# When the bias rows, exponents, mask pieces and last sources of a ranked graph propagation are issued

## The chip, the cores and the metric

The kernel runs on one core of a Trainium2 chip. The metric is device time in microseconds (us) of one execution. One execution is also recorded by the hardware profiler, and its page and trace are the evidence that is read here.

Engines are named as in the profile: PE is TensorE's matmuls, PEld its weight loads, DVE is VectorE, ACT is ScalarE, POOL is GpSimd, and SP is SyncE, which only issues loads here. Each engine takes its own instructions in order; between engines there are semaphores.

## The reference, cut to what matters

A graph of N = 3327 nodes has a sparse, weighted, symmetric-pattern adjacency matrix A (3327 x 3327, f32) and node features x (3327 x 64). Four residual layers follow one another, each `x = x + f(relu(layernorm(x)))`. In all, A or a matrix made from it multiplies a 64-wide array eight times; I call these propagations k = 0 to 7.

- Layer 0, k = 0 and 1: two gated graph steps, each A times features, then a GRU cell.
- Layer 1, k = 2: each nonzero is replaced by a power of one half that depends on its rank in its row:

```
mask = (adj != 0)
rank = cumsum(mask, axis=1); deg = rank[:, -1:]
k = minimum(deg, 100); pos = rank - (deg - k)
w = mask * where(pos > 0, 0.5 ** (k - pos), 0)
out = w @ (input @ weight) + bias
```

- Layer 2, k = 3, 4, 5: the weights are A squared element by element; each step is `x = (w @ x) @ W.T + b`.
- Layer 3, k = 6 and 7: plain A again, with a small dense step and a tanh.

## The kernel before, in words

**Tiles and chunks.** The targets are cut into four chunks of 384, 384, 384 and 512 columns per half (`CH`), two halves each. Chunks 0 and 1 are group 0, chunks 2 and 3 are group 1 (`GROUPS`). A tile holds 128 sources against all targets of one group: 128 x 2 x 384 columns a chunk, 768 KB in group 0 and 896 KB in group 1. Twenty slots hold tiles; SP loads them from HBM in the order of use, each as soon as its slot is free. A is read anew for every pair of propagations.

**Units.** A list of units (k, chunk, tile) is written out by the functions `alone` and `joint`: group 0 at k = 0; group 1 at k = 0 and 1; group 0 at k = 1 and 2; group 1 at k = 2 and 3; and so on. `joint(g, k, sweep, later, keep)` lets the second propagation follow the first: a tile is used for k and, `later` tiles afterwards, for k + 1. The function `run` plays the list. Ahead of a unit's matmuls it issues loads, the preparation of tiles (squares for k = 3 to 5, L404 on ACT), the exponents of the ranked units (`expand`, three units ahead), and mask pieces.

**A ranked unit (k = 2).** A tile's mask is made by two "pieces" on DVE (L427: adj != 0, as bf16, one per half), and POOL fetches one row of totals into it by DMA (L432). PE multiplies the mask by a triangle of ones (L271, `tri`), which gives ranks in a PSUM bank, one for each of the two halves s. ACT (L482) or DVE (L480) turns a bank into a bf16 power of two, `e`, and frees the bank; the choice is `on_vector`. PE then does L566: six matmuls, three bf16 terms of y by two halves. The last piece of a tile frees the tile's slot, and so releases a load.

**Last sources.** Each 128-source tile loses its last source to the totals row. Those 26 sources are handled once per group by `last_sources(g)`: POOL clears a half slot (L523), SP loads 26 rows for each half (two L527), DVE forms the mask and subtracts totals (L529, L533), and ACT makes the exponents (L535). They are used by a unit called `SPECIAL`, the last k = 2 unit of a chunk. The two runs of `last_sources` are tasks that start 70 and 140 us into the planner's own time.

**Tasks.** What follows a finished sum is a generator with a planned delay at each `yield`: `spend` lets time pass as units are issued, `advance` takes one step, `finish` takes all that are left. After k = 1 comes `gru`, which sets y[2] and, 80 planned us later in group 1 (14 in group 0), adds a row of biases to xs (`add_row`, L802). After k = 2 comes `after_2`: evacuate the sum (L711 on DVE or L709 on ACT), a dense step on PE (L271 with `bd`), add to xs (L796), layernorm (L774 to L776 and L782, L783 on DVE, L779 squares on ACT, L785 power on POOL, L789 on DVE, which sets y[3]), and 15 planned us later another `add_row`. The corresponding steps of the layer before are L794 (residual), L781 and L859 to L868 (splitting y into three bf16 terms).

**The order around the change.** A `SPECIAL` unit needs y of all chunks. It therefore finishes the tasks of all other chunks before its matmuls, also what their `yield`s would have left for later. The pieces are spread by `run`: in k = 2, one per unit in group 1, none while group 0 works on its own sources, except every third unit once y[2] of group 0 is there.

Of the kernel before, what the change touches and what calls it, by code (L numbers as in the profile page):

```python
# [52 lines left out]
NC = 4  # L53
PARTS = (4, 5)
CWM = 512
GROUPS = [(0, 1), (2, 3)]
# [23 lines left out]
SPECIAL = None  # L80
# [16 lines left out]
def kernel(  # L97
# [165 lines left out]
    def width(c):  # L263
        return blocks(c) * P
# [60 lines left out]
    def begin(c, task):  # L325
        finish(c)
        tasks[c] = [task, 0.0]
        advance(c)

    def finish(c):  # L330
        while c in tasks:
            advance(c)

    def later_task(us, task):
        yield us
        yield from task
# [10 lines left out]
    y = [[None] * NC for _ in range(8)]  # L347
# [54 lines left out]
    def square(sq, v, turn):  # L402
        if turn % 3 or any(ch in tasks or (2, ch) in sums for ch in range(NC)):
            nc.scalar.activation(sq, v, AF.Square)  # L404
        else:
            nc.vector.tensor_tensor(sq, v, v, ALU.mult)  # L406

    def prepare(k, c, t):

        if t is SPECIAL:  # L410
            return
        kind = KIND[k] if k != COUNT else COUNT
        if kind in (RANKED, COUNT) and t.mask is None:
            make_mask(t, kind)
        if kind == SQUARED and t.in_place and c not in t.squares:
            t.squares.add(c)
            square(t.view(c), t.view(c), t.q + c)

    pieces = deque()

    def make_mask(t, kind):

# [15 lines left out]
    def mask_pieces(n=0, t=None):  # L438

        while pieces and (n > 0 or any(u is t for u, _, _ in pieces)):  # L440
            _, half, piece = pieces.popleft()
            piece(half)
            n -= 1

    def expand(k, c, t):

        if k == COUNT:
            return None
        w = width(c)
        if t is SPECIAL:  # L450
            g = c // 2
            w0 = (CH[c][0] - CH[GROUPS[g][0]][0]) * P
            finish(NC + 1 + g)
            return lastw[g][:, w0:w0 + w].bitcast(BF16)
        if KIND[k] == PLAIN or (KIND[k] == SQUARED and t.in_place):
            return t.view(c)
        if KIND[k] == SQUARED:
            room = Mask(t.w)
            wide = room.view.rearrange("p s w -> p (s w)").bitcast(F32)[:, :2 * w].rearrange("p (s w) -> p s w", s=2)
            square(wide, t.view(c), t.q + c)  # L460
            squared[k, c, t] = room
            return wide
        wide = work.tile([P, 2, CWM], I16, name="e", bufs=4)[:, :, :w]

        mask_pieces(t=t)
        for s in range(2):
            i, ps = take()  # L470
            mm(ps[:, :w], tri, t.mask.view[:, s, t.cols(c)])
            own = chunk_of(t.q % NB) in GROUPS[t.g]
            busy = any((k - 1, ch) in sums for ch in GROUPS[t.g])
            if t.g == 1 and not own and any(y[3][ch] is None for ch in GROUPS[0]):

                on_vector = s and c == GROUPS[1][1]
            else:
                on_vector = s and (own if t.g == 0 and (own or busy) else c == GROUPS[t.g][1] or t.g == 1 and not own)
            if on_vector:
                nc.vector.tensor_scalar(wide[:, s], ps[:, :w], BITS, 0.0, op0=ALU.add, op1=ALU.max)  # L480
            else:
                nc.scalar.activation(wide[:, s], ps[:, :w], AF.Relu, bias=bitsb)  # L482
            give(i)
        spend(STREAM_US * w / CWM * 0.5)
        if c == GROUPS[t.g][1]:
            t.mask.free()
        return wide.bitcast(BF16)
# [29 lines left out]
    def last_sources(g):  # L517

        w = sum(width(c) for c in GROUPS[g])
        w0 = CH[GROUPS[g][0]][0] * P  # L520
        room = Mask(w)
        v = room.view.rearrange("p s w -> p (s w)").bitcast(F32)
        nc.gpsimd.memset(v, 0.0)  # L523
        yield 4.0
        rows = adjT.rearrange("(q p) (s n) -> q p s n", p=P, s=2)
        for s in range(2):
            nc.sync.dma_start(out=v[s * D:s * D + NQ], in_=rows[:, P - 1, s, w0:w0 + w])  # L527
        yield 12.0
        nc.vector.tensor_scalar(v, v, 0.0, 129.0 * TWO7, op0=ALU.not_equal, op1=ALU.mult)  # L529
        for c in GROUPS[g]:  # L530
            finish(("count", c))
        yield 1.0
        nc.vector.scalar_tensor_tensor(v, totals[g], -TWO7, v, op0=ALU.mult, op1=ALU.add)  # L533
        yield 1.5
        nc.scalar.activation(lastw[g], v, AF.Relu, bias=bitsb)  # L535
        room.free()

    def propagate(k, c, t, rhs, first, last):
        if k == COUNT:
            count(t, first, last)  # L540
            return
        w = width(c)
        if first:
            sums[k, c] = [take(sums=True) for _ in range(2 if k == 7 and c == PARTS[1] else 1)]
            sums[k, c] = [sums[k, c][0], sums[k, c][-1]]
        acc = sums[k, c]
        if t is SPECIAL:
            for ch in range(NC):
                if ch != c:
                    finish(ch)  # L550
            terms = [[lasty[:, h, i, :] for h in range(2)] for i in range(3)]
            rhs = [rhs, rhs]
        else:
            s, b = divmod(t.q, NB)
            cs = chunk_of(b)
            if y[k][cs] is None:
                finish(cs)
            terms = [[yk[:, b - CH[cs][0], s, :]] * 2 for yk in (y[k][cs] if KIND[k] == RANKED else [y[k][cs]])]
            rhs = [rhs[:, h, :] for h in range(2)]
            if KIND[k] != RANKED:  # L560
                t.used()
            if (k, c, t) in squared:
                squared.pop((k, c, t)).free()
        for n, yq in enumerate(terms):
            for h in range(2):
                nc.tensor.matmul(acc[h][1][h * D:(h + 1) * D, :w], yq[h], rhs[h], start=first and n == 0,  # L566
                                 stop=last and n == len(terms) - 1)
        if t is not SPECIAL and t.early and t.mask is None:
            make_mask(t, RANKED)
        spend(STREAM_US * w / CWM * (0.75 if KIND[k] == RANKED else 1.0))  # L570
        if last:
            begin(c, after[k](c, sums.pop((k, c))))
# [97 lines left out]
    def run():  # L670
        total = {}
        for k, c, t in units:
            total[k, c] = total.get((k, c), 0) + 1
        done = {}
        loaded, masked, prepared, expanded = 0, 0, 0, deque()
        for i, (k, c, t) in enumerate(units):
            while loaded < len(units) and loaded < i + LOAD:
                u = units[loaded][2]
                if u is not SPECIAL and u.slot is None:
                    if len(dead) <= RESERVE and loaded > i + EXPAND:  # L680
                        break
                    u.load()
                loaded += 1
            while masked < min(loaded, i + MASK):
                if is_masked(*units[masked]):
                    if not spare and len(dead) <= RESERVE + 1:
                        break
                    make_mask(units[masked][2], RANKED)
                masked += 1
            while prepared < min(loaded, i + PREPARE):  # L690
                prepare(*units[prepared])
                prepared += 1
            while len(expanded) < min(EXPAND + 1, len(units) - i):
                assert prepared > i + len(expanded)
                expanded.append(expand(*units[i + len(expanded)]))
            if k != 2:
                mask_pieces(1 + len(pieces) // 6)
            elif not (c in GROUPS[0] and (t is SPECIAL or chunk_of(t.q % NB) in GROUPS[0])):
                mask_pieces(1)
            elif i % 3 == 0 and all(y[2][ch] is not None for ch in GROUPS[0]):  # L700
                mask_pieces(1)
            n = done[k, c] = done.get((k, c), 0) + 1
            propagate(k, c, t, expanded.popleft(), n == 1, n == total[k, c])

# [260 lines left out]
    alone(0, 0, sweep=2, lag=5)  # L965
    joint(1, 0, sweep=6, later=4, keep=3, lag=2)
    joint(0, 1, sweep=4, later=20, keep=0)
    joint(1, 2, sweep=6, later=5, keep=1)
    joint(0, 3, sweep=8, later=4, keep=4)
    joint(1, 4, sweep=8, later=4, keep=4)  # L970
    joint(0, 5, sweep=8, later=4, keep=4)
# [6 lines left out]
        else:  # L978
            begin(c, before_0(c))
    begin(NC, more_constants())  # L980
    begin(NC + 1, later_task(70.0, last_sources(0)))
    begin(NC + 2, later_task(140.0, last_sources(1)))
    run()
    for c in list(tasks):
        finish(c)
# [39 lines left out]
```

## Time and profile before

The median of three runs is 712.32 us (712.25 to 713.13).

| what | value |
|---|---|
| profiled execution | 712.98 us |
| span of its trace | 710.9 us |
| mean granted PE clock | 0.999 |
| PE busy | 682.9 us, 96% of the span |
| DVE busy | 338.7 us, 48% |
| ACT busy | 267.4 us, 38% |
| POOL busy | 79.5 us, 11% |
| HBM read | 199.45 MB, 282 GB/s over the span |

Busy shares by stage, from the windows of the trace (us busy of the stretch):

| stretch, us | what runs | PE | DVE | ACT | DMA share |
|---|---|---|---|---|---|
| 200 to 220 | group 0, k = 1 ends; GRU cells begin | 19.75 | 17.62 | 10.31 | 0.95 |
| 220 to 240 | group 0, k = 2; GRU cells | 19.64 | 17.28 | 15.01 | 0.90 |
| 240 to 260 | group 0, k = 2 | 19.93 | 16.51 | 15.99 | 0.56 |
| 260 to 280 | group 1, k = 2 begins; after_2 of chunks 0 and 1 | 17.13 | 17.54 | 12.98 | 0.44 |
| 280 to 300 | group 1, k = 2 and 3 | 17.97 | 15.71 | 16.37 | 0.52 |
| 380 to 620 | k = 3 to 6 | 240.00 of 240 | 72.87 | 84.59 | 0.80 |

How to read it: ends of matmuls are modelled, so PE's busy time is an upper view of it, and what matters is where PE starts late. L numbers are lines of the kernel before. In the trace's lines the tiles of the PSUM banks are called `sum` and `temp`, whatever they hold.

### The profile page before, as it was taken

The page shows a single profiled execution, that of the slowest core. Times are in us where ns is not written, and L with a number is a line of the kernel's source. Part 1 is how long each engine was busy: PE and PEld are TensorE (multiplying, and loading weights), DVE is VectorE, ACT ScalarE, POOL GpSimd, SP SyncE. Part 2 cuts the span into 40 slices and gives each one's busy share as a digit, 9 for nine tenths or more (in the row PEclk, how much of TensorE's full clock was granted, in tenths as well). Part 3 has the DMA queues.
Part 4 walks back from the last instruction along what each step waited for, and adds up shares of the span by engine and source line. Part 5 has one row for each costly group of instructions (what it writes and reads, how often), then busy time and mean ns, then how long its engine had stood idle before and what let it go on. Part 6 is the DMA issues. An engine that isn't in the chain of part 4 may idle for free.

```text
span 710.9 us, 12617 instructions
## 1 busy us (share of the span) xinstructions
PE 682.9 (96%) x5128; PEld 353.9 (50%) x5128; DVE 338.7 (48%) x692; ACT 267.4 (38%) x411; POOL 79.5 (11%) x114
## 2 busy tenths in 40 slices
PE   1999999999999998999999999999999999999997
PEld 1454666643546785446444444334444444334464
DVE  7456826643997888747533103221271565005101
ACT  1014100122137868788997224740166600000101
POOL 4300000001383414011100000000010000000000
PEclk9999999999999999999999999999999999999999
DMA  9999995189699833682799659962997399927991
GB/s 343 401 388 405 405 401 175 53 319 395 197 326 324 290 123 106 236 282 90 271 372 348 233 175 409 406 239 94 385 366 266 111 390 405 405 80 270 404 401 38
DMA packets 68549, 201.31 MB, mean 283 GB/s; under 512 B 7228, under 2 KB 8228, under 8 KB 68492
## 3 DMA queue, kind: packets, MB, share of 16 engines
q1 hardware_dynamic: 65596, 199.46, 75.9%
q8 instruction: 40, 0.66, 0.4%
q10 hardware_dynamic: 720, 0.85, 0.3%
q0 software_dynamic: 2176, 0.20, 0.2%
q14 instruction: 17, 0.14, 0.1%
HBM read 199.45 MB, written 0.85 MB: 282 GB/s over the span
## 4 chain that ended last, share of the span: by engine, by line
PE 57%; DVE 3%; DMA 1%; ACT 1%; issue 0%; POOL 0%; ACTq 0%; DVEq 0%; POOLq 0%; SPq 0%
PE sum L566 53%; PE temp L271 3%; PE temp L730 1%; DMA adj<-in_adjT 1%; DVE e L480 1%; DVE adj L427 1%; POOL st L785 0%; DVE both L765 0%; ACT both L764 0%; DVE st L774 0%; ACT e L482 0%; DVE xs L796 0%; PE sum L271 0%; DVE st L782 0%; ACT adj L404 0%
## 5 line engine op out<-in xcount | busy, mean ns | idle before, releaser
L566 PE MATMUL sum<-adj,y 128*64 128x384 f32 (+3 forms) x3016 | 532.4, 502 | 3.1 <-DVE e L480 1.6
L566 PEld LDWEIGHTS sum<-adj,y 128*64 128x64 f32 x3016 | 228.8, 137 | 251.0 <-issue 222.3
L404 ACT ACTIVATE adj<-adj 128x768 f32<-128x768 f32 (+1 forms) x174 | 142.7, 891 | 49.6 <-PE sum L566 23.9
L427 DVE TENSOR_SCALAR adj<-adj 128x768 bf16<-128x768 f32 (+3 forms) x208 | 113.3, 593 | 39.0 <-PE temp L501 35.0
L566 PE MATMUL sum<-e,both 128*64 128x384 bf16 (+1 forms) x624 | 73.1, 339 | 0.4 <-DVE e L480 0.2
L482 ACT ACTIVATE e<-temp,bitsb 128x384 int16<-128x384 f32 (+1 forms) x117 | 66.2, 607 | 18.6 <-PE temp L271 13.5
L764 ACT COPY both<-sum 64x384 f32<-64x384 f32 (+3 forms) x17 | 8.1, 477 | 150.3 <-PE sum L566 150.3
L765 DVE COPY both<-sum 64x384 f32<-64x384 f32 (+3 forms) x17 | 9.7, 568 | 114.6 <-ACT both L764 113.4
L406 DVE TENSOR_TENSOR adj<-adj 128x768 f32<-128x768 f32 (+1 forms) x34 | 32.6, 1008 | 53.3 <-DMA adj<-in_adjT 31.0
L785 POOL TENSOR_TENSOR st<-st,mhalf 128x6 f32<-128x6 f32 (+1 forms) x16 | 24.3, 1516 | 291.1 <-DVE st L783 291.1
L271 PE MATMUL temp<-adj,tri 128*64 128x384 bf16 (+1 forms) x334 | 50.8, 341 | 0.2
L432 POOL DMA_DIRECT2D adj<-totals x52 | 37.0, 714 | 124.3 <-DMA adj<-in_adjT 74.8
L566 PEld LDWEIGHTS <-both 128*64 128x64 bf16 x624 | 40.6, 110 | 19.2 <-issue 6.7
L480 DVE TENSOR_SCALAR e<-temp 128x384 int16<-128x384 f32 (+1 forms) x50 | 30.5, 611 | 21.1 <-PE temp L271 9.8
L271 PEld LDWEIGHTS <-tri 128*64 128x64 bf16 x416 | 28.1, 110 | 17.9 <-issue 10.0
L759 DVE STREAM_TRANSPOSE both<-y 32x96 f32<-32x96 f32 (+1 forms) x128 | 35.6, 278 | 2.9
L711 DVE COPY t<-sum 128x384 f32<-128x384 f32 x8 | 4.4, 556 | 61.2 <-PE sum L566 61.2
L501 PE MATMUL temp<-adj,behind 128*64 128x384 bf16 x208 | 30.1, 339 | 0.9 <-DVE adj L427 0.7
L501 PEld LDWEIGHTS <-behind 128*64 128x64 bf16 x208 | 16.8, 110 | 17.7 <-issue 16.5
L709 ACT COPY t<-sum 128x384 f32<-128x384 f32 (+1 forms) x8 | 4.2, 528 | 53.9 <-PE sum L566 53.9
L921 DVE TENSOR_TENSOR y<-temp,brow 128x384 f32<-128x384 f32 (+1 forms) x8 | 4.7, 591 | 29.6 <-PE temp L271 29.6
L535 ACT ACTIVATE lastw<-adj,bitsb 128x768 int16<-128x768 f32 (+1 forms) x2 | 2.0, 990 | 44.7 <-DVE adj L533 44.7
(121 smaller groups left out, 329.2 us busy)
## 6 DMA issues: line engine op xcount, KB each, us to landing
adj<-in_adjT SPq DMA_DIRECT2D x130, 768.0 KB, 8.9
adj<-in_adjT SPq DMA_DIRECT2D x104, 896.0 KB, 11.1
xs<-in_x SPq DMA_DIRECT2D x1, 640.0 KB, 4.2
adj<-totals POOLq DMA_DIRECT2D x26, 3.0 KB, 5.7
adj<-totals POOLq DMA_DIRECT2D x26, 3.5 KB, 3.1
out<-xs ACTq DMA_DIRECT2D x2, 192.0 KB
out<-xs ACTq DMA_DIRECT2D x1, 256.0 KB, 6.7
stage<-in_weights SPq DMA_DIRECT2D x2, 112.0 KB, 14.3
```

Of the source, the lines that this page charges most:

```text
L271: nc.tensor.matmul(out[hs], lhsT[:, hs], rhs, start=start, stop=stop)
L404: nc.scalar.activation(sq, v, AF.Square)
L406: nc.vector.tensor_tensor(sq, v, v, ALU.mult)
L427: nc.vector.tensor_scalar(t.mask.view[:rows, half], t.view()[:rows, half], 0.0, None, op0=ALU.not_equal)
L432: nc.gpsimd.dma_start(out=t.mask.view[P - 1:P], in_=totals[t.g][t.q:t.q + D + 1:D, :])
L480: nc.vector.tensor_scalar(wide[:, s], ps[:, :w], BITS, 0.0, op0=ALU.add, op1=ALU.max)
L482: nc.scalar.activation(wide[:, s], ps[:, :w], AF.Relu, bias=bitsb)
L501: nc.tensor.matmul(counts[c][1][s * D:(s + 1) * D, :w], behind[:, NQ - 1 - t.q:NQ - 1 - t.q + D], t.mask.view[:, s, t.cols(c)], start=firs ...
L566: nc.tensor.matmul(acc[h][1][h * D:(h + 1) * D, :w], yq[h], rhs[h], start=first and n == 0, stop=last and n == len(terms) - 1)
L759: nc.vector.transpose(to[at:at + 32, :, q], h[q * 32:(q + 1) * 32, :, s, f * 32:(f + 1) * 32])
L765: nc.vector.tensor_copy(both[c][upper(1), 1], acc[1][1][upper(1), :width(c)])
L785: nc.gpsimd.tensor_tensor(st[:, 3, :n], st[:, 2, :n], mhalf[:, :n], ALU.pow)
```

## The change

1. `SPECIAL`: instead of finishing all tasks of the other chunks, each chunk's task is advanced only until its y is set. The bias rows (`add_row`) are left to their planned time.
2. Exponents: a flag `relief["squares"]` is set when the first in-place squares are issued, and takes the place of the test on y[3] of group 0. A flag `relief["pieces"]` is set for the own ranked units of group 0 after y[2] of that group is there; while it is set, an s = 1 bank goes to DVE unless (q + c) is divisible by 4.
3. In those units a piece is issued every second unit, not every third.
4. `joint(1, 2)`: k = 3 follows k = 2 six tiles later, not five.
5. `last_sources` begin at 130 and 155 of planned time, not 70 and 140.

```diff
@@ prepare
         if kind == SQUARED and t.in_place and c not in t.squares:
             t.squares.add(c)
+            relief["squares"] = True
             square(t.view(c), t.view(c), t.q + c)
 
     pieces = deque()
+
+    relief = {"squares": False, "pieces": False}
@@ expand
-            if t.g == 1 and not own and any(y[3][ch] is None for ch in GROUPS[0]):
+            if t.g == 1 and not own and not relief["squares"]:
 
                 on_vector = s and c == GROUPS[1][1]
+            elif relief["pieces"]:
+                on_vector = s and (t.q + c) % 4
             else:
@@ propagate
         if t is SPECIAL:
             for ch in range(NC):
-                if ch != c:
-                    finish(ch)
+                while y[k][ch] is None:
+                    advance(ch)
@@ run
+            relief["pieces"] = False
             if k != 2:
                 mask_pieces(1 + len(pieces) // 6)
             elif not (c in GROUPS[0] and (t is SPECIAL or chunk_of(t.q % NB) in GROUPS[0])):
                 mask_pieces(1)
-            elif i % 3 == 0 and all(y[2][ch] is not None for ch in GROUPS[0]):
-                mask_pieces(1)
+            elif all(y[2][ch] is not None for ch in GROUPS[0]):
+                relief["pieces"] = t is not SPECIAL
+                if i % 2 == 0:
+                    mask_pieces(1)
@@ the list of units and tasks
-    joint(1, 2, sweep=6, later=5, keep=1)
+    joint(1, 2, sweep=6, later=6, keep=1)
-    begin(NC + 1, later_task(70.0, last_sources(0)))
-    begin(NC + 2, later_task(140.0, last_sources(1)))
+    begin(NC + 1, later_task(130.0, last_sources(0)))
+    begin(NC + 2, later_task(155.0, last_sources(1)))
```

## The prediction

> **What bounds the kernel now.** I read the page's busy times first, then what TensorE (PE) waits for, then PE, DVE, ACT and the DMA queue in order of time in the stretches where PE waits.
>
> ```profile
> PE 682.9 (96%) x5128; PEld 353.9 (50%) x5128; DVE 338.7 (48%) x692; ACT 267.4 (38%) x411; POOL 79.5 (11%) x114
> ```
>
> PE carries the kernel: a gain is lost PE time won back. Ends of matmuls are modelled, so I count losses from starts: six bf16 matmuls of 384 columns follow one another in 0.49 us (287.20 to 287.69), four f32 ones in 0.64 (289.09 to 289.73). A start later than that spacing allows is lost time. Over the execution this gives some 20 us beside the 14.9 of the first wait; 380 to 620 us lose nothing, 120 to 345 us lose about 12. The waits for PE:
>
> ```profile
> PE temp L747 <- DVE y L789: 14.9, 1, 14.9
> PE sum L271 <- DVE e L480: 2.1, 2, 1.1
> PE sum L566 <- DVE e L480: 1.8, 2, 1.6
> PE sum L566 <- DMA adj<-in_adjT: 0.9, 2, 0.7
> ...
> PE temp L271 <- DVE t L711: 0.8, 1, 0.8
> ```
>
> Columns: total, times, longest. Apart from the first, the large ones belong to DVE in the ranked pass (k=2), and one to a load. By spacing: 0.83 at 130.41 (load), 0.37 at 212.89 (load), 0.95 at 264.18 (L711), 1.24 at 273.44, 1.23 at 278.62, 0.49 at 280.95, 0.43 at 282.75, 1.81 at 286.29 (exponents, L480 and L482). What DVE does before them (start, duration, work, wait before it):
>
> ```profile
> 262.41 1.16 DVE L802 TENSOR_TENSOR xs<-xs,brow 128x384 f32<-128x384 f32 x2
> 263.48 0.55 DVE L711 COPY t<-sum 128x384 f32<-128x384 f32 x1
> ...
> 271.75 0.56 DVE L789 SCALAR_TENSOR_TENSOR y<-t,st 128x384 f32<-128x384 f32 x1 [1.54 <-POOL st L785]
> 272.23 0.55 DVE L802 TENSOR_TENSOR xs<-xs,brow 128x384 f32<-128x384 f32 x1
> 272.70 0.68 DVE L480 TENSOR_SCALAR e<-sum 128x512 int16<-128x512 f32 x1
> ...
> 277.88 0.68 DVE L480 TENSOR_SCALAR e<-sum 128x512 int16<-128x512 f32 x1
> ...
> 285.55 0.68 DVE L480 TENSOR_SCALAR e<-sum 128x512 int16<-128x512 f32 x1
> ```
>
> Three bias additions (L802) and a layernorm end (L789), none of them urgent, stand ahead of L711 and L480, which PE awaits. L711's sum was complete at 261.79, the rank product for 272.70 at 269.33.
>
> **What the Trainium skill says.** "Perfetto Trace Analysis", Identifying the Most-Contended Engine, holds matmul busy share a poor measure of nearness to the limit; the trace agrees: 96% covers a busy figure that includes modelled ends. Its section Optimization Strategy says to find the gaps of the bounding engine by stage and what posts their semaphore: that is the list above. Its section Matmuls wants independent groups rotated through PSUM banks so that evacuation overlaps; here the rotation is what fails, since PE waits at 273.44 and 278.62 for a bank that L480 has not emptied. "DMA: Bandwidth & Descriptors", Issuing engines are not separate DMA queues, has all issuers share 16 DMA engines; the trace agrees where it matters: 407 GB/s and a share of 1.04 in 205 to 210 us.
>
> **The change part by part.**
>
> *Last sources' rows, first group, later.* Its two L527 loads leave 97 us for about 172, and the half slot with them. The last four 896-wide loads before 130 us then start when their slots come free (98 to 119) and land by about 124.7, where the late one landed at 130.36. The 0.83 at 130.41 goes. Its L529 and L533 (about 0.53 and 0.95 us to the next start) now fall at 200 to 202 us, in a full DVE (4.96 of 5 us in 200 to 205), ahead of the pieces L427 that free slots for the last 768-wide loads. The last of these is issued at 205.76 after a piece at 205.15, so up to 1.5 us later; but DMA is backlogged until it lands at 212.8 and has two 91 KB loads less, and PE comes 0.83 earlier. Bounds of the loss there: 0 (backlog covers all) to 1.5 (landing moves with the piece). I take 0.3.
>
> *Second group later.* Its L527 pair goes behind the 768-wide loads and holds SP until POOL's memset (L523, queued behind the copies L868 to 216 us). Queued behind are 896-wide loads (208.48 to 219.38 before) first read by pieces at 250: cover of 25 us, cost nothing; uncovered it would be up to 8 us. L529 and L533 leave 209 to 211.5 for here:
>
> ```profile
> 229.81 0.56 DVE L843 TENSOR_TENSOR adj<-adj 128x384 f32<-128x384 f32 x1
> ...
> 232.13 0.55 DVE L480 TENSOR_SCALAR e<-sum 128x384 int16<-128x384 f32 x1
> ...
> 233.85 0.56 DVE L480 TENSOR_SCALAR e<-temp 128x384 int16<-128x384 f32 x1
> 234.33 0.55 DVE L794 SCALAR_TENSOR_TENSOR xs<-temp,xs 128x384 f32<-128x384 f32 x1
> ```
>
> DVE has no gap, and PE starts 0.05 or 0.06 us after the ends of the L480 at 232.13, 233.85 and 236.18 and the L794. L529 (0.54) goes in before 228.06, where 0.22 of waiting and rounding absorb 0.3: +0.24. L533 (1.0) goes in after 232.13 and passes whole to PE at 234.47: +1.0. ACT's L535 (1.04) waits for it and blocks ACT from 232.8 to 234.9; the L482 behind it are late by 1.7 against banks that PE, itself 1.24 late, asks for at least 0.4 later: nothing. Sum +1.24; bounds 0.2 (L533 absorbed) and 2.3 (L535 adds its 1.04).
>
> *Exponents shared.* Four L480 of 384 between 253 and 260 us move to ACT as L482 (0.47 each to the next start). PE spends 0.813 us per 384-wide unit there, and ACT starts within 0.1 of its input; each moved one makes ACT at most 0.5 late, and banks come round after more than 1. Cost nothing; uncovered, 4 x 0.47.
>
> *Pieces every second unit.* They use the DVE time freed: five L427 of 896 (0.53 each) come into 250 to 265 us and leave 265 to 291. POOL gets two L432 before each L785, whose inputs PE finished at 260: nothing.
>
> *Bias rows not forced.* The L802 at 262.41, 262.88 and 272.23 (0.47, 0.60, 0.47) go to 295 to 303 us, where DVE is a third idle. Now DVE in the new order, with the start-to-start times of the old one (L480 0.47 or 0.60, L427 0.53, L796, L774 and L782 0.58, L776 and L789 0.48):
> - L711 starts at 262.41, ends at 262.97; PE comes at 263.23. 0.95 gone.
> - Two L480, the added L427, L480, L427, L796, L774 to L776, L480, L427, L782, L783: the L480 of 272.70 starts at 269.2, ends at 269.9. PE, 0.95 earlier, asks at 271.25. 1.24 gone.
> - Two L427, L480 (rank product 270.93), L427, L789 (POOL done by 271.4), L796, L774 to L776, L427: the L480 of 277.88 starts at 275.0, ends at 275.7. PE asks at 278.62 - 1.23 - 2.19 = 275.2. 0.55 of 1.23 stays; together 2.87 gone.
> - Up to 285.55 two L427 fewer stand between. L480 start at 277.3, 279.0, 280.6, 281.6 and 283.8. PE's order there has the first tile of k=3 one tile later (the 6 for 5; squared pass: ACT's L404 for it one place later, done at 279.9, used at 283.3). PE waits 0.42, 0.78, 0.27 and 0.45, in all 1.92 for 2.73 before: 0.8 gone.
>
> L789 now meets DVE at 272.1 instead of 270.2. It waits for POOL's L785 (1.35 us in the first layernorm, 2.07 in the second, and begun at 269.3), so its old wait of 1.54 is filled with exponents and pieces. Should POOL be 1 us later, L789 holds up L796, the second chunk's layernorm and the L480 of 277.88 behind it by that much, which is inside the bounds; the y it writes is first read by PE at 283.
>
> In all -3.7. Bounds: -1.6 if DVE stays full and only part of the removed work shows, -4.5 if the new order hides more. From 318 us PE's order is as before, loads and squares are released by PE, and the gain stays.
>
> Sum on the profiled execution, 712.98 (span 710.9 and 2.1 around it): -0.83 + 0.3 + 1.24 - 3.7 = -3.0, or 710.0. The median of the runs stood 0.66 below it: 709.3.
>
> **Rivals.**
> 1. The stalls re-form: the load's gain is given back at 212.89 (+0.83), and DVE, still full from 262 to 290, yields 2.2. Sum -0.83 + 0.83 + 1.24 - 2.2 = -0.1, or 712.2. For it: DVE is busy 17.5 of 20 us in 260 to 280. Against: that holds 1.54 us of L802 that leave. 0.17.
> 2. All covers hold: L533 absorbed and 262 to 290 wins 4.5: about -5, or 707.3. Against: the 0.05 us at three starts. 0.08.
> 3. Slower: ACT becomes the bound in the squares. It runs L404 without a gap from 342.31 to 367, and PE takes a square at 358.44 that ended at 356.90: a lead of 1.54. ACT has gained 4 x 0.47 + 1.04 = 2.9 us after 228. If idle ACT time before 338 absorbs under 1.54 of this, PE waits there; with none, the earlier gain is lost and 2.9 - 1.54 = 1.4 more: 713.7. Against: ACT idles 7.0 us in 260 to 280 and 3.6 in 280 to 300, and its block is released by PE. 0.15.
>
> **How the numbers follow.** The forecast has 0.60, its own range 708.0 to 711.5. Faster or slower by over 0.2% (1.4 us) is about what a measurement can tell. Faster: 0.56 of the forecast's 0.60, 0.08 of rival 2, 0.05 of rival 1: 0.69. Slower: 0.15. Same: 0.16. The range 707.5 to 712.9 leaves out most of rival 3 and a part of rival 2.
>
> **What would show it.** Right: no wait for a load at 130; PE waiting for L480 or L794 near 234 about 1.2 longer; L711 directly after L427 near 262 and no wait for L789 on DVE near 271; PE's waits for L480 in 270 to 290 about half. Wrong: a load wait of 1 us or more at 212, PE waiting for ACT's L404 near 358, or L480 in 270 to 290 as late as before.

## The result and the profile after

The changed kernel takes 709.74 us (median of 6 runs, 708.99 to 710.67), beside 712.17 us for the kernel before (6 runs, 711.73 to 713.13). The ratio is 0.9965, 95% interval 0.9952 to 0.9978: faster by 0.35%, an interval that leaves out 1, and 0.4 us from the forecast. The profiled execution of the changed kernel took 709.73 us, with a span of 707.8 beside 710.9.

Of these 3.1 us between the two spans, 0.9 belong to neither kernel. PE begins its first sums at about 16 us, and in both profiles its f32 matmuls start in pairs, one pair every 0.64 us at first and every 0.32 later. In the profile before this turns at 20.1 us, in the one after at 18.2, so that PE of the changed kernel is 0.9 us ahead at 21 us, before any part of the change acts. The two profiles of the kernel before differ there too, by 0.5 us.

Line numbers of the changed kernel are 3 to 8 higher: L427, L480, L482, L529, L533, L566, L711, L789, L794, L802 became L430, L485, L487, L534, L538, L571, L719, L797, L802, L810. From here on L802 in a line of the changed kernel is the old L794.

What PE waits for between 200 and 300 us in the changed kernel (total, times, longest):

```profile
PE temp L271 <- DVE e L485: 1.2, 2, 0.9
PE sum L571 <- DMA adj<-in_adjT: 0.8, 1, 0.8
PE sum L271 <- DVE e L485: 0.7, 2, 0.4
PE sum L571 <- DVE e L485: 0.6, 2, 0.5
PE sum L271 <- DVE adj L836: 0.2, 1, 0.2
```

The wait for L711 is gone, the 2.1 and 1.8 us for L480 are down to 0.7 and 0.6, and two waits have come: 1.2 for an L485 of a `temp` bank, and 0.8 for a load. By starts, as in the prediction, PE's lost time is:

| place in the kernel before | before | after |
|---|---|---|
| load near 130 | 0.83 | 0 |
| near 207 (205 to 206 in the changed kernel), new: exponents late behind L534 and L538 | 0 | 0.11 + 0.21 |
| load near 212 | 0.37 | 1.03 |
| 232 to 235: banks behind L534 and L538 | 0 + 0.10 | 0.33 + 1.10 |
| 264, L711 | 0.95 | 0 |
| 273, L480 | 1.24 | 0 |
| 278, L480 | 1.23 | 0.61 |
| 280 to 287 | 0.49 + 0.43 + 1.81 | 0.43 + 0.69 + 0.29 + 0.45 |

The last four rows are the stretch that the change is aimed at: 6.15 us before, 2.47 after. I call this sum the loss of the ranked stretch below. DVE of the changed kernel in that stretch (start, duration, work):

```profile
262.40 0.62 DVE L430 TENSOR_SCALAR adj<-adj 127x896 bf16<-127x896 f32 x1
262.93 0.55 DVE L719 COPY t<-sum 128x384 f32<-128x384 f32 x1
...
269.67 0.68 DVE L485 TENSOR_SCALAR e<-sum 128x512 int16<-128x512 f32 x1
...
272.73 0.54 DVE L797 SCALAR_TENSOR_TENSOR y<-t,st 128x384 f32<-128x384 f32 x1
...
275.57 0.68 DVE L485 TENSOR_SCALAR e<-sum 128x512 int16<-128x512 f32 x1
...
282.19 0.68 DVE L485 TENSOR_SCALAR e<-sum 128x512 int16<-128x512 f32 x1
```

L719 follows the piece directly, L797 no longer shows a wait for POOL, and the three L485 that stood at 272.70, 277.88 and 285.55 begin 3.0, 2.3 and 3.4 us earlier. PE reached this stretch 0.5 us later than before (263.75 for 263.23, where it would have started without its wait) and was 3.2 us earlier when it had passed it (316.39 for 319.58, the same matmul).

### The profile page after: what moved, and what is told of

The parts are those of the page before. It is cut to its first block, busy times and chain, and to the rows that moved or that the text cites. A ratio compares the mean times of both kernels' runs of the same rounds, so it can differ in the third digit from the quotient of the medians.

```text
span 707.8 us, 12613 instructions
## 1 busy us (share of the span) xinstructions
PE 682.0 (96%) x5128; PEld 354.7 (50%) x5128; DVE 338.3 (48%) x688; ACT 268.3 (38%) x415; POOL 76.1 (11%) x114
## 4 chain that ended last, share of the span: by engine, by line
PE 56%; DMA 1%; DVE 1%; ACT 0%; issue 0%; POOL 0%; ACTq 0%; DVEq 0%; SPq 0%; POOLq 0%
PE sum L571 52%; PE temp L271 3%; PE temp L738 1%; DMA adj<-in_adjT 1%; DMA out<-xs 1%; DVE both L773 0%; ACT both L772 0%; POOL st L793 0%; DVE xs L966 0%; ACT t L963 0%; DVE e L485 0%; PE sum L271 0%; ACT t L717 0%; DVE y L797 0%; DVE y L789 0%
## 5 line engine op out<-in xcount | busy, mean ns | idle before, releaser
L571 PE MATMUL sum<-adj,y 128*64 128x384 f32 (+3 forms) x3016 | 532.0, 501 | 1.6 <-DMA adj<-in_adjT 0.8
L571 PEld LDWEIGHTS sum<-adj,y 128*64 128x64 f32 x3016 | 229.1, 137 | 248.2 <-issue 222.6
L404 ACT ACTIVATE adj<-adj 128x768 f32<-128x768 f32 (+1 forms) x174 | 142.6, 891 | 49.0 <-PE sum L571 25.0
L430 DVE TENSOR_SCALAR adj<-adj 128x768 bf16<-128x768 f32 (+3 forms) x208 | 114.7, 600 | 39.2 <-PE temp L506 31.2
L571 PE MATMUL sum<-e,both 128*64 128x384 bf16 (+1 forms) x624 | 73.6, 339 | 0.5 <-DVE e L485 0.5
L487 ACT ACTIVATE e<-temp,bitsb 128x384 int16<-128x384 f32 (+1 forms) x120 | 67.4, 607 | 14.1 <-PE temp L271 8.3
L406 DVE TENSOR_TENSOR adj<-adj 128x768 f32<-128x768 f32 (+1 forms) x34 | 32.6, 1009 | 53.9 <-DMA adj<-in_adjT 31.6
L571 PEld LDWEIGHTS <-both 128*64 128x64 bf16 x624 | 41.0, 110 | 19.3 <-issue 7.0
L435 POOL DMA_DIRECT2D adj<-totals x52 | 33.1, 638 | 51.5 <-PE temp L271 49.1
L485 DVE TENSOR_SCALAR e<-temp 128x384 int16<-128x384 f32 (+1 forms) x46 | 28.3, 617 | 20.8 <-ACT e L487 10.9
L719 DVE COPY t<-sum 128x384 f32<-128x384 f32 x8 | 4.4, 556 | 60.5 <-PE sum L571 60.5
L824 PE MATMUL temp<-both,cells 128*64 128x384 f32 (+1 forms) x68 | 17.2, 520 | 0.0
```

The lines of the kernel that those rows point to most:

```text
L430: nc.vector.tensor_scalar(t.mask.view[:rows, half], t.view()[:rows, half], 0.0, None, op0=ALU.not_equal)
L435: nc.gpsimd.dma_start(out=t.mask.view[P - 1:P], in_=totals[t.g][t.q:t.q + D + 1:D, :])
L824: nc.tensor.matmul(ps[upper(1 - s), :w], cells[:, cell, s, g, :], both[c][:, s], start=True, stop=True)
```

## Experiments

All medians are of runs beside the kernel before on the same chip, and ratios are to it; its own median was 712.2 to 712.3 in each set, so medians of different sets can be compared to a few tenths. The loss of the ranked stretch comes from the profile of each.

**The bias rows alone.** Theory: the forced bias additions and the early L789 make the waits. Rival: relieving DVE by exponents and pieces does it.

```diff
 (kernel before)
-                if ch != c:
-                    finish(ch)
+                while y[k][ch] is None:
+                    advance(ch)
```

> The kernel before with only the SPECIAL unit's rule changed: other chunks' tasks are advanced until y is set, no longer finished. Theory (the forced bias rows L802 and the L789 behind them made the waits of 264 to 279 us): PE's lost time at 264 and 273 goes (2.2 us) and about half of that at 278 (0.7), so about -2.9 us against before, some 709.3; DVE no longer waits 1.5 us for POOL near 271. Rival (the gain comes from relieving DVE by exponents on ACT and earlier pieces): only the first wait goes, about -1 us, 711.2.

Measured: 709.62 us, ratio 0.9965 (0.9953 to 0.9977). PE's loss of the ranked stretch falls from 6.15 to 3.37. DVE in this kernel, in the old line numbers:

```profile
261.88 0.55 DVE L711 COPY t<-sum 128x384 f32<-128x384 f32 x1
...
268.62 0.68 DVE L480 TENSOR_SCALAR e<-sum 128x512 int16<-128x512 f32 x1
...
271.68 0.54 DVE L789 SCALAR_TENSOR_TENSOR y<-t,st 128x384 f32<-128x384 f32 x1
```

The waits at 264 and 273 are gone and 0.62 of 1.23 stays at 278. This one edit, which does not touch the order of the loads, is worth as much as the whole change nets. The rival falls.

**The last sources alone.**

```diff
 (kernel before)
-    begin(NC + 1, later_task(70.0, last_sources(0)))
-    begin(NC + 2, later_task(140.0, last_sources(1)))
+    begin(NC + 1, later_task(130.0, last_sources(0)))
+    begin(NC + 2, later_task(155.0, last_sources(1)))
```

> The kernel before with only the two last_sources tasks begun at 130 and 155 instead of 70 and 140 of planned time. Theory: the load wait of 0.83 us at 130 goes, two thirds of it come back as a load wait near 212 (1.0 instead of 0.4), and L529 and L533 in the full stretch of DVE near 232 cost PE 1.3 us; in all about +1.1 us, 713.3. Rival (moving them is a gain, since the slot and the SP queue are freed earlier): -0.8 us or better, 711.4.

Measured: 713.54 us, ratio 1.0017 (1.0010 to 1.0023): slower, by 1.4 us. PE loses 0.33 at 231.61 and 1.10 at 234.34, where the kernel before loses nothing and 0.1. The load wait near 212 was only 0.24 this time, so that part of the expectation missed: see the loads below.

A second cost of the later sources was in no expectation. In all six profiles that have them PE loses 0.32 us between 204 and 208 us, and in none of the seven with the sources as before. Here the first group's L534 and L538 stand ahead of L869 (the old L861), which splits y. DVE in the changed kernel:

```profile
198.20 0.55 DVE L534 TENSOR_SCALAR adj<-adj 128x768 f32<-128x768 f32 x1
...
200.95 0.95 DVE L538 SCALAR_TENSOR_TENSOR adj<-totals,adj 128x768 f32<-128x768 bf16 x1
...
202.76 0.68 DVE L869 TENSOR_TENSOR y<-y,both 128x512 f32<-128x512 f32 x1
```

The two take 0.47 and 0.87 us to the next start, 1.34 together. ACT's cast waits for this L869, and its exponents follow the cast. In the kernel before, the exponents that PE needed at 206.66 and 207.46 had ended 1.2 and 1.0 us earlier; in the changed kernel they end at 205.04 and 205.98, and PE starts 0.05 us after each. No run moved the first group's sources alone; the one below that moves only the second group's keeps the 0.32.

**Exponents and pieces alone.** The flags that these lines read are set as in the change; the other three parts are as before.

```diff
 (kernel before)
-            if t.g == 1 and not own and any(y[3][ch] is None for ch in GROUPS[0]):
+            if t.g == 1 and not own and not relief["squares"]:
...
+            elif relief["pieces"]:
+                on_vector = s and (t.q + c) % 4
...
-            elif i % 3 == 0 and all(y[2][ch] is not None for ch in GROUPS[0]):
-                mask_pieces(1)
+            elif all(y[2][ch] is not None for ch in GROUPS[0]):
+                relief["pieces"] = t is not SPECIAL
+                if i % 2 == 0:
+                    mask_pieces(1)
```

> The kernel before with only the exponents' choice of engine and the pieces of every second unit changed (bias rows, last sources and the 5 tiles as before). Theory: DVE has two or three L427 fewer before 286, so of the waits after 278 about 0.5 to 1 us goes, while those at 264 and 273 stay: about -0.7 us, 711.5. Rival (this relief of DVE is the main gain): -2.5 us, 709.7.

Measured: 712.38 us, ratio 1.0006 (0.9998 to 1.0014): no difference. Both theory and rival missed. The loss of the ranked stretch is 6.65, not less than 6.15: the waits at 264, 273 and 278 are unchanged, and the last one is 2.06 for 1.81. (The profiled run is the slowest of the 14, 714.21, with a load wait of 2.01 near 212, ahead of this stretch.)

**The changed kernel with five tiles.**

```diff
 (changed kernel)
-    joint(1, 2, sweep=6, later=6, keep=1)
+    joint(1, 2, sweep=6, later=5, keep=1)
```

> The changed kernel with k = 3 following k = 2 by five tiles again, not six. Theory: the first k = 3 tile's bank wait near 285 comes back in part, 0.3 to 0.8 us slower than the changed kernel, about 710.2. Rival (the sixth tile does nothing): as the changed kernel, 709.7.

Measured: 711.38 us, ratio 0.9992 (0.9985 to 0.9998). Taking the sixth tile back costs 1.6 us by the medians and 1.4 by the loss of the ranked stretch (3.84 for 2.47): twice the most that I had expected. The wait before the first f32 matmuls on 512 columns is 2.06.

**The sixth tile alone.**

```diff
 (kernel before)
-    joint(1, 2, sweep=6, later=5, keep=1)
+    joint(1, 2, sweep=6, later=6, keep=1)
```

> The kernel before with only k = 3 six tiles after k = 2 in place of five. Theory (the sixth tile gives DVE one more pair of ranked units before PE needs the first bank for k = 3, whatever DVE did before): the 1.81 us at 286 fall to about 0.5 while the three waits of 264 to 279 stay, so about -1 us in all after what shifts to 280 to 284: 711.2. Rival (the sixth tile pays only once the bias rows are out of the way): 712.2.

Measured: 711.27 us, ratio 0.9988 (0.9980 to 0.9996). The loss of the ranked stretch is 5.28: 0.95, 1.24 and 1.23 are as before, and 2.73 after 280 became 1.86. The rival falls.

**Bias rows and sixth tile, nothing else.** The two diffs together, on the kernel before.

> The kernel before with two parts of the change only: the SPECIAL rule and k = 3 six tiles after k = 2. Theory (these two are the gain; exponents and pieces cost 0.5 us, the last sources 1.3): the bias rule's 2.8 us of won PE time plus 1.4 for the sixth tile, so about -4 us against before, 708.1, and PE's lost time of 260 to 290 near 2 us. Rival (the sixth tile pays only together with the exponents and pieces): as the bias rule alone, 709.6.

Measured: 708.69 us, ratio 0.9953 (0.9940 to 0.9966). The loss of the ranked stretch is 2.49, with the same five waits as the changed kernel (0.62, 0.44, 0.69, 0.29, 0.45). So these two parts are the whole gain there, and the rival falls. I had counted the exponents and pieces as a cost of 0.5, after the last two runs; with six tiles they cost nothing.

A count on DVE fits this. Between the L480 that begins at 277.88 in the kernel before and the one at 285.55 stand eight L427; eight also in the kernels with the bias rule alone, with exponents and pieces alone, and in the changed one with five tiles; six in the four kernels with six tiles that I counted (the changed one, the sixth tile alone, with the bias rule, and with the sources at 230). The pieces that the new rule issues earlier do not thin out this interval. One tile of f32 matmuls fewer on PE does, since fewer units, and so fewer pieces, are issued between the two: the interval is 7.67 us with eight and 6.62 with six, shorter by about two L427 of 0.53. That the two pieces alone are the sixth tile's gain is not shown, since PE's own order changes with it.

**The changed kernel with its last sources where they were.**

```diff
 (changed kernel)
-    begin(NC + 1, later_task(130.0, last_sources(0)))
-    begin(NC + 2, later_task(155.0, last_sources(1)))
+    begin(NC + 1, later_task(70.0, last_sources(0)))
+    begin(NC + 2, later_task(140.0, last_sources(1)))
```

> The changed kernel with the two last_sources tasks begun at 70 and 140 again. Theory: the 1.4 us that L529 and L533 cost PE near 232 come back: 708.4. Rival (the later sources pay for themselves by the load waits at 130 and 212): 709.7 or slower.

Measured: 709.00 us, ratio 0.9952 (0.9938 to 0.9966). The waits near 232 and 235 are gone, and so is the loss near 206; load waits of 0.40 at 130 and 0.39 at 212 stand in its profile. Of the 1.4 us only 0.7 shows in the medians: between theory and rival, with an interval of the ratio (1 us to either side) that reaches both. This kernel and the one with bias rows and sixth tile differ in exponents and pieces alone, and were run in one set: 709.00 and 708.69, no difference.

**The second group's last sources out of the full stretch.**

```diff
 (changed kernel)
-    begin(NC + 2, later_task(155.0, last_sources(1)))
+    begin(NC + 2, later_task(230.0, last_sources(1)))
```

> The changed kernel with only the second group's last_sources begun at 230 instead of 155 of planned time, so that its DVE work falls near 315 us, where DVE has room. Theory: the waits near 232 and 235 lose 1.4 us, nothing else moves: 708.4. Rival (it is SP's queue or the memset, not the two DVE instructions, that costs): 709.7.

Measured: 708.30 us, ratio 0.9947 (0.9934 to 0.9960), 1.4 us under the changed kernel, as the theory says. PE's loss at 232 and 235 is as in the kernel before. The memset, the loads and ACT's L540 move with the two DVE instructions, so the run alone does not tell them apart; the lines do. The two run where DVE has room:

```profile
306.15 0.62 DVE L534 TENSOR_SCALAR adj<-adj 128x896 f32<-128x896 f32 x1
...
309.99 1.08 DVE L538 SCALAR_TENSOR_TENSOR adj<-totals,adj 128x896 f32<-128x896 bf16 x1
```

while in the changed kernel the first stands at 226.95 in a DVE without a gap, and the second between two exponents that PE waits for. DVE of the changed kernel, and then PE of it with its waits in brackets:

```profile
231.65 0.55 DVE L485 TENSOR_SCALAR e<-sum 128x384 int16<-128x384 f32 x1
232.12 1.08 DVE L538 SCALAR_TENSOR_TENSOR adj<-totals,adj 128x896 f32<-128x896 bf16 x1
...
234.37 0.56 DVE L485 TENSOR_SCALAR e<-temp 128x384 int16<-128x384 f32 x1
```

```profile
232.26 0.35 PE L271 MATMUL sum<-adj,tri 128*64 128x384 bf16 x2 [0.29 <-DVE e L485]
234.99 0.82 PE L271 MATMUL temp<-adj,tri 128*64 128x384 bf16 x4 [0.91 <-DVE e L485]
```

**The kernel before, profiled again.**

> The kernel before, unchanged, profiled once more. Theory (the load waits near 130 and 212 vary from execution to execution): other values than 0.83 and 0.37 us there, while the waits from 264 to 286 are the same to 0.1 us. Rival (the load waits belong to the order of the loads): the same values again.

Measured: 712.81 us in one execution. The waits of 264 to 286 are the same to 0.01 us (0.95, 1.24, 1.24, 0.49, 0.43, 1.81). The load wait is 0.54 at 130 and nothing near 212. Over all profiles, in us of PE's lost time (0: under 0.18):

| loads | near 130 | near 212 |
|---|---|---|
| as before (7 profiles) | 0.83, 0.54, 0, 0.23, 0.34, 0.40, 0.82 | 0.37, 0, 0, 2.01, 0.60, 0.39, 0 |
| last sources later (6 profiles) | 0 in all | 1.03, 0.24, 0.35, 0, 0, 0 |

Near 130 the later sources do remove a wait, worth 0.45 us on average: in the profiles looked at for this, SP issued the last load at about 118 instead of 125 us. Near 212 the wait comes and goes with either order; why one landing is late and the next is not, none of these runs tells.

**No pieces during the layernorms.** An attempt at the rest of the loss. Both of the next kernels have the second group's sources at 230.

```diff
             elif not (c in GROUPS[0] and (t is SPECIAL or chunk_of(t.q % NB) in GROUPS[0])):
-                mask_pieces(1)
+                if c in GROUPS[0] or all(y[3][ch] is not None for ch in GROUPS[0]):
+                    mask_pieces(1)
```

> The changed kernel with the second group's last sources at 230 of planned time, and with no mask pieces issued in group 1 while y[3] of group 0 is not there, that is during the two layernorms. Theory (what is left of PE's waits from 275 to 285, 2.5 us, is DVE's time for L427 that nothing needs yet): most of it goes, 706.5. Rival (the pieces come due at once, and DVE is as late a few tiles on): 708.3, with waits for DVE after 285.

Measured: 709.01 us, ratio 0.9956 (0.9942 to 0.9969). The rival holds in kind; the waits come sooner than the 285 us that it names. PE waits for the pieces themselves:

```profile
275.75 0.35 PE L271 MATMUL sum<-adj,tri 128*64 128x384 bf16 x2 [1.21 <-DVE adj L430]
279.04 0.35 PE L271 MATMUL temp<-adj,tri 128*64 128x384 bf16 x2 [1.37 <-DVE adj L430]
```

All waits for L485 in the stretch are gone, and 3.3 us for L430 stand in their place. The last piece had been issued at 267.16, so the lead of ready masks lasted 8.6 us.

**Half the pieces during the layernorms.**

```diff
-                if c in GROUPS[0] or all(y[3][ch] is not None for ch in GROUPS[0]):
+                if c in GROUPS[0] or i % 2 == 0 or all(y[3][ch] is not None for ch in GROUPS[0]):
```

> As the kernel with the second group's last sources at 230, but in group 1 a piece only every second unit, not none, until y[3] of group 0 is there. Theory (the lead of pieces lasted about 10 us without any, so it lasts some 20 at half the rate, past both layernorms): the waits for L485 from 275 to 285 fall from 2.5 to about 1 us and none for L430 comes, 707.0. Rival (any piece held back is missed within these tiles): 708.3 or slower, with PE waiting for L430.

Measured: 706.60 us (705.89 to 707.09), ratio 0.9921 (0.9908 to 0.9935): the fastest of all, 3.1 us under the changed kernel. What PE still waits for from 200 to 300 us in it, in full:

```profile
PE sum L571 <- ACT e L487: 0.3, 1, 0.3
PE sum L271 <- DVE adj L837: 0.2, 1, 0.2
```

The loss of the ranked stretch is 0.75. Between the two L480 of the count above only four pieces are left.

## Why the prediction was right, step by step

The forecast was 709.3, the measured median 709.74. Term by term:

- *The load wait at 130* (-0.83): right in cause, too large. The profile that I priced it by was the highest of seven. The average is 0.45.
- *The load wait near 212* (+0.3, between 0 and 1.5): not supported. The changed kernel's profile shows +0.66, in the range that I gave, but kernels with the loads of before show 0 to 2.01, and those with the later sources 0 to 1.03. I had named a load wait of 1 us or more at 212 as a sign of being wrong, and the changed kernel's profile has one of 1.03. Over all profiles it does not belong to the change: four of the six kernels with the later sources have 0.24 or less there.
- *The first group's sources on DVE* (no term): I looked at what L534 and L538 do to the last loads, and not at the exponents behind them. They cost 0.32 near 206.
- *The second group's sources on DVE* (+1.24): right in place and cause. PE's work behind them moved by 0.34 and 1.00, in all 1.34 (the 1.43 by starts holds the 0.1 that was there before). The difference is L534, with 0.63 to the next start for my 0.54. That ACT's part and the hold of the SP queue would cost nothing, held: moving all of it away returned 1.4 us and no more.
- *The ranked stretch* (-3.7): measured 6.15 - 2.47 = 3.68. Place by place: 0.95 and 1.24 gone as said; 0.61 left for 0.55; then 0.43, 0.69, 0.29, 0.45 for 0.42, 0.78, 0.27, 0.45. The walk along DVE in the new order, with start-to-start times of the old one, was good to 0.1 us at each wait. Its starts are some 0.5 us early, by as much as PE came later into the stretch.

With 0.45 near 130, no term near 212, +0.32, +1.34 and -3.68 the sum is -2.5; measured was -2.4. That the forecast came so near is in part luck: the 0.3 near 212 has no support, and the 0.32 near 206, which I had left out, stands in its place.

What the prediction had wrong inside a right term is the attribution. "Pieces every second unit" was said to bring five L427 into 250 to 265 us and take them out of 265 to 291; it is three (6 to 9, and 20 to 17). The bias rows' bullet counted two L427 fewer before 285.55; the count shows that these two belong to the sixth tile. The exponents' move and the earlier pieces are worth nothing: 712.38 alone, and equal waits with and without them (2.47 and 2.49). The medians of single parts against the kernel before, 2.6 faster (bias), 1.1 faster (sixth tile), 0.2 slower (exponents and pieces, inside the noise) and 1.4 slower (sources), add to 2.1 faster, beside 2.4 for all together.

The rivals. Rival 1 has an error in its sum: -0.83 + 0.83 + 1.24 - 2.2 is -0.96, not -0.1, and so 711.4, which lies inside the forecast's own range. The median could hardly have told the two apart; the places do. The stalls did not re-form in the ranked stretch, which yielded 3.68 and not 2.2; half of the one at 278 stays (0.61). In rival 2 the cover of L533 did not hold, as the starts 0.05 us after DVE's ends had said. ACT did not become the bound: no profile shows PE waiting for L404 near 358, and from 300 to 620 us PE loses no more than before. The share of 1.04 and the 407 GB/s that the prediction gives for 205 to 210 us show full DMA engines; they do not show that several issuers share them.

## What to carry to other kernels

When one engine works ahead in a fixed order, look not at its busy share but at what stands ahead of the instruction that the bounding engine awaits; three additions and the end of a layernorm, none needed yet, cost 2.8 us of PE's starts here (2.6 by the medians). Work that is put off needs a place where the engine has gaps: the same two instructions cost 1.4 us at 232 and nothing at 306. Stock that is made ahead (masks) may be thinned while the maker is busy, but only as far as the lead lasts: beside the kernel with the sources at 230, half the rate won 1.7 us where none at all lost 0.7.

## What was not expected of the hardware

The waits for engines repeat to 0.01 us between two profiles of one kernel, those for loads do not: PE lost 0.83 and 0.54 us at one tile and 0.37 and 0 at another. Over seven profiles with the same order of loads it was 0 to 0.83 and 0 to 2.01. Here a load wait read from one profile is a draw, not a size.

The start scatters as well. The matmul that PE begins as its hundred and first, the same in all kernels, starts between 29.9 and 31.6 us over the 13 profiles, in no order that follows the changes (31.1 and 31.6 in the two of the kernel before), because PE's f32 matmuls take up their faster spacing sooner in one execution than in another. Spans of two single profiles are therefore no measure of a change of 1 us; waits place by place are.
